# Order of the chunk work, PSUM tiles and side work in the first layer of a two-layer graph attention kernel

## Chip, cores and metric

The kernel runs on one core of a Trainium2 chip. The metric is the device time of one execution in microseconds (us), lower being better. A profile of a single execution is shown beside the timed runs; its times are those of that execution alone.

## What is computed

Two attention layers over 8 graphs of 2048 nodes with 256 features and 4 heads. Both layers normalise the rows, apply a ReLU, attend over the adjacency matrix and add the input back. The change concerns layer 0 only. Cut to what matters there:

```python
h = relu(layernorm(x))
q, k, v = (h @ W.T + b).reshape(B, N, H, 64)            # per head
kc, vc = k, v in chunks of 256 keys                      # 8 chunks
scores = clip(q @ kc.T / 8, -10, 10)
scores = where(mask == 0, -10, scores)
attn = softmax(scores, axis=-1)                          # over the 256 keys of ONE chunk
ctx = sum over chunks of attn @ vc
out = layernorm(ctx @ Wo.T + bo + h) * gamma + beta
x = x + out
```

The softmax is taken inside each chunk, so each chunk needs its own row sums before its context can be added up.

## The kernel before, in words

**Chunk steps.** Layer 0 is one loop (L701) over 256 steps n: 8 batches b, 4 query blocks qb of 512 rows, 8 chunks c of 256 keys. A chunk has four score tiles (two key tiles of 128 times two head pairs), each 128 keys by 2 heads by 512 queries. The loop is software-pipelined and written out by hand (`manual_schedule`, L87): every engine executes its instructions in the order in which Python emits them. In step n the scores of step n + 2 are made, the sums of step n + 1 and the contexts of step n.

**One score tile** (`scores`, L396): two matmuls with 64 rows of contraction, one per head, which share the array by rows (form 64\*128 in the profile), into one of two PSUM pairs of the tag "big" (two banks each). DVE then clips and masks the tile into SBUF (L409), and ACT exponentiates it (L415).

**Contexts** (`weigh`, L417): for a key tile and a half (`part`) of the value columns four matmuls with 32 output columns, one per head, which share the array by columns (form 128\*32). They accumulate over the two key tiles in the PSUM tile "both" (two banks, one per part).

**Sums**: GpSimd (POOL) adds the exponentials of the two key tiles (L695), four 128\*32 matmuls with a column of ones sum them over the partitions (`add_up`, L429) into the PSUM tile "sums". `divide` (L436) copies them with ACT to SBUF and sends them by DMA (SP queue) into a compact shape; `spread` (L444) takes the reciprocal on DVE and sends it through DRAM to all partitions as r. `accumulate` (L454) multiplies both by r on DVE (one instruction for both parts), and POOL adds the product to acc.

**Order in a step**: two score tiles, their exponentials; `advance` (only for n < 7); contexts of the first key tile; `advance`; two more score tiles; sums of step n + 1; contexts of the second key tile; last exponential and POOL's two sums; accumulate; spread; `advance`.

**Side work** hangs in generators in the list `aside`. One `advance` (L207) goes through the list and takes one piece of each generator, until a piece returns None, which marks work of TensorE in an "aux" PSUM tile. A piece that yields True has emitted something else, False means that it waits for its step. `drain` advances until a condition holds. The generators are:
- `make_limit` (L237), in the first steps: the adjacency matrix, loaded, cast and transposed on TensorE into the mask `limit`.
- `block` (L282), once for each 512 rows of a batch: `normal` (ACT makes h from x, L155), `turn` (four transposes on TensorE, form 128\*128, L167, and a copy to hT on ACT, L175), twice; then two aux tiles each for q, k, v (L164). The numbers in its `while` lines are the earliest steps.
- `statistics` (L131): the x blocks of a whole batch are loaded, and DVE takes row statistics (L47, L48); then each block is loaded a second time by `ahead`.
- `finish` (L461), for each query block: ACT makes h again (L472), the product with Wo in two aux tiles, DVE adds and row statistics, ACT (L506) and POOL (L475, L517) normalise and add, one POOL operation a step; a DMA stores x1.
- In the last batch `preparation` (L556) for layer 1, and `fill`.

PSUM before: big 2 pairs (4 banks), both (2), sums (1), aux (1).

Layer 1 (from L855) runs 512 rounds; its tiles `near` use the tag big, its row sums `den` the bank of sums.

Of the kernel before, what the change touches and what calls it, by code (L numbers as in the profile page):

```python
# [51 lines left out]
def layers(  # L52
# [36 lines left out]
    early, turns = [True], [0]  # L89

    def aux(dtype=F32):

        n = QB if dtype == F32 else 2 * QB
        turns[0] += 1
        if early[0] and turns[0] % 2:
            return psum.tile([P, 2 * n], dtype, tag="both", name="aux")[:, :n]
        return psum.tile([P, n], dtype, tag="aux", name="aux")
# [32 lines left out]

    def statistics(rows):  # L131

        rstd, off = norms()
        mv = small.tile([P, NKT, 2], F32, tag="mv", name="mv", bufs=1)
        for blk, xb in enumerate(ahead(rows)):
            if blk == 0:
                yield True
                yield True
            for t in range(NT):
                row_stats(nc, small, mv[:, blk * NT + t, :], xb[:, t, :])  # L140
                if t % 2:
                    yield True
        roots(mv, rstd, off, slice(0, NKT))
        yield True
        yield True
        return rstd, off
# [135 lines left out]
    def block(b, blk, xb, qs, ks, vs):  # L282
# [3 lines left out]
        while b and here[0] < first + (NCH, 2 * NCH, 3 * NCH, 4 * NCH - 2)[blk]:  # L286
            yield False
        while b == 1 and len(made) < NQB:
            yield False
        if b and blk == 0:  # L290
            yield True
        hT = big.tile([P, FC, QB], F32, tag="hT", name="hT", bufs=1)
        yield from block_turned(xb, blk, norm_of[b], hT)
        for name, to in (("q", qs), ("k", ks)):
# [4 lines left out]
            for oc in range(FC):  # L299
# [12 lines left out]
                if oc == FC - 1:  # L312
                    to.append(r)
                yield
        while b and here[0] < first + (0, 0, 3 * NCH + 2, 3 * NCH + 4)[blk]:
            yield False
        r = big.tile([P, NT, F], F32, tag="kv", name="v", bufs=12)
        for two in range(NT // 2):
            nc.scalar.copy(r[:, 2 * two : 2 * two + 2, :], sides(wT["v"], two, hT))
            if two == 1:  # L320
                vs.append(r)
            yield

    def batch(b):
        qkv[b] = ([], [], [])
        if b == 0:
            rstd, off = norms()
            mv = small.tile([P, NKT, 2], F32, tag="mv", name="mv", bufs=1)
            norm_of[b] = rstd, off
            for blk, xb in enumerate(ahead(x[b])):  # L330
                if blk == 0:
                    yield True
                for t in range(NT):
                    row_stats(nc, small, mv[:, blk * NT + t, :], xb[:, t, :])
                of = slice(blk * NT, (blk + 1) * NT)
                roots(mv, rstd, off, of)
                yield from block(b, blk, xb, *qkv[b])
        else:
            norm_of[b] = yield from statistics(x[b])
            for blk, xb in enumerate(ahead(x[b])):  # L340
                yield from block(b, blk, xb, *qkv[b])
# [54 lines left out]
    def scores(qb, kt, hp, qs, ks):  # L396

        ps = psum.tile([P, 2, QB], F32, tag="big", name="big", bufs=2)
# [55 lines left out]
    def accumulate(acc, both, r, first):  # L454

        to = acc if first else heads_tile("c", "c")
        nc.vector.tensor_tensor(to, both, bcast(r, 1, 2), ALU.mult)  # L457
        if not first:
            nc.gpsimd.tensor_tensor(acc, acc, to, ALU.add)  # L459
# [218 lines left out]
    def prepared(step):  # L678
# [3 lines left out]
        drain(lambda: qb in made and b in qkv and len(qkv[b][1]) > c // 2)  # L682
        qs, ks, _ = qkv[b]
        first = [scores(qb, 2 * c, hp, qs, ks) for hp in range(2)]
        for e in first:
            exponential(e)
        yield first
        second = [scores(qb, 2 * c + 1, hp, qs, ks) for hp in range(2)]
        exponential(second[0])
        yield second  # L690
        exponential(second[1])
        added = []
        for hp in range(2):
            both = heads_tile("add", "add")
            nc.gpsimd.tensor_tensor(both, first[hp], second[hp], ALU.add)  # L695
            added.append(both)
# [4 lines left out]
    for n in range(-2, len(steps)):  # L701
        here[0] = n
        more = n < NCH - 1
        coming = prepared(steps[n + 2]) if n + 2 < len(steps) else iter(())
        inside = -1 <= n < len(steps) - 1
        if n >= 0:
# [3 lines left out]
            if (qb, c) == (0, 2) and b + 1 < B:  # L710
# [4 lines left out]
            early[0] = False  # L715
            both = psum.tile([P, 2, QB], F32, tag="both", name="both")
        for k in range(2):
            weights.setdefault(n + 2, []).append(next(coming, None))
            if more:
                advance()  # L720
            if k == 1 and inside:
                sums = psum.tile([P, QB], F32, tag="sums", name="sums")
                add_up(weights[n + 1][2], sums)
                got = divide(sums)
            if n >= 0:
                weigh(2 * c + k, 0, weights[n][k], qkv[b][2], both, k == 0)
            if n >= 0:
                weigh(2 * c + k, 1, weights[n][k], qkv[b][2], both, k == 0)
            if k == 1:
                weights[n + 2].append(next(coming, None))  # L730
                if n >= 0:
                    if c == 0:
# [484 lines left out]
```

## Time and profile before

| what | us |
|---|---|
| median of 3 runs | 4355.52 (4352.07 to 4357.29) |
| the profiled execution, its own time | 4354.15 |
| its span, first to last instruction | 4352.4 |
| from the first row sum (L432) to the last product (L457) | 111.7 to 2842.9 |
| layer 1, from its first matmul (L786) | 2848.2 to the end |

| engine | busy us | share of the span |
|---|---|---|
| TensorE matmul (PE) | 4160.7 | 96% |
| GpSimd (POOL) | 3388.4 | 78% |
| VectorE (DVE) | 3188.1 | 73% |
| ScalarE (ACT) | 2522.3 | 58% |
| TensorE weight load (PEld) | 1364.8 | 31% |

A line of the profile names the engine, the line of the code, the operation, the tile it writes and the tiles it reads, the form of a matmul (rows\*columns of the array), the shape, and how often; then busy time and the mean of one. In the timeline the first number is the start in us from the span's start, the second the length, and a bracket holds idle time ahead of it and who ended it. An fp32 matmul appears as two instructions, each with its weight load. TensorE's matmuls overlap, so their starts say more than their lengths. A matmul of 512 columns starts 0.43 us after the one before it in the same part of the array.

### The profile page before, as it was taken

Reading aid. Unit: us, or ns where it says so; the run is one execution under the profiler, and the core shown is the slowest. Engines: PE = TensorE matmul, PEld = TensorE weight load, DVE = VectorE, ACT = ScalarE, POOL = GpSimd, SP = SyncE. Lnnn points to the kernel's source line nnn. Section 1 sums busy time; section 2 is a strip of 40 time slices with the busy share of each in tenths; the row PEclk is TensorE's granted clock in tenths of the full one; section 3 lists DMA queues with packets and bytes.
Section 4 is the critical chain, followed back from the end, with each engine's and each line's share of the span. In section 5 each row is a group of like instructions: output and inputs, shape, how many; then the busy total and the mean of one; then the engine's idle time right before and its main releaser. Section 6 shows DMA issues by size and latency. Waiting matters only on the chain. (4 is left out here: it accounts for less than half of the span.)

```text
span 4352.4 us, 85973 instructions
## 1 busy us (share of the span) xinstructions
PE 4160.7 (96%) x34742; PEld 1364.8 (31%) x34742; DVE 3188.1 (73%) x3718; ACT 2522.3 (58%) x3194; POOL 3388.4 (78%) x1711
## 2 busy tenths in 40 slices
PE   6799999999999999999999999989999999999998
PEld 2233323323323323333333323323333232333322
DVE  3876666676676675676676667679888898989897
ACT  4455555555555555555555557655656656566665
POOL 0477787787787777887877788888888888888897
PEclk9899999999999999999999999999999999999999
DMA  2321122121121121121121112122221212122121
GB/s 72 125 79 46 41 61 58 37 65 54 41 66 46 48 66 42 46 63 51 42 67 52 41 49 60 39 79 57 60 62 48 69 44 78 50 61 69 32 59 35
DMA packets 278152, 246.03 MB, mean 57 GB/s; under 512 B 95728, under 2 KB 228592, under 8 KB 277744
## 3 DMA queue, kind: packets, MB, share of 16 engines
q1 hardware_dynamic: 273136, 223.67, 18.2%
q0 software_dynamic: 4608, 16.78, 1.0%
q8 instruction: 274, 4.49, 0.4%
q14 instruction: 134, 1.10, 0.1%
HBM read 202.05 MB, written 36.18 MB: 55 GB/s over the span
## 5 line engine op out<-in xcount | busy, mean ns | idle before, releaser
L695 POOL TENSOR_TENSOR add<-E 128x1024 f32<-128x1024 f32 x512 | 1204.0, 2374 | 617.2 <-ACT E L415 562.8
L415 ACT ACTIVATE E<-E 128x1024 f32<-128x1024 f32 x1024 | 1081.6, 1058 | 970.7 <-DVE E L409 942.5
L409 DVE SCALAR_TENSOR_TENSOR E<-big,limit 128x1024 f32<-128x1024 f32 x1024 | 1199.1, 1212 | 444.3 <-PE big L401 325.7
L775 DVE SCALAR_TENSOR_TENSOR e<-near,far,limit 128x1024 f32<-128x1024 f32 x1024 | 1239.8, 1277 | 40.3 <-POOL t L892 19.4
L892 POOL TENSOR_TENSOR t<-t,e 128x1024 f32<-128x1024 f32 x448 | 1054.9, 2389 | 222.0 <-ACT t L888 185.2
L401 PE MATMUL big<-qT,kT 64*128 64x512 f32 x4096 | 1042.1, 623 | 33.6 <-DVE E L409 33.4
L786 PE MATMUL acc<-e,qn 128*32 128x512 f32 x8192 | 1041.3, 597 | 6.9 <-DVE e L775 6.7
L421 PE MATMUL both<-E,v 128*32 128x512 f32 x8192 | 990.5, 597 | 0.2 <-DVE c L457 0.2
L888 ACT ACTIVATE t<-e,quot 128x1024 f32<-128x1024 f32 x512 | 561.8, 1142 | 275.0 <-PE den L798 166.2
L401 PEld LDWEIGHTS big<-qT,kT 64*128 64x128 f32 x4096 | 350.6, 187 | 621.2 <-issue 360.5
L459 POOL TENSOR_TENSOR acc<-acc,c 128x1024 f32<-128x1024 f32 x224 | 533.4, 2381 | 2.7 <-DVE c L457 2.7
L457 DVE TENSOR_TENSOR c<-both,r 128x1024 f32<-128x1024 f32 x224 | 274.3, 1224 | 243.7 <-PE both L421 129.0
L421 PEld LDWEIGHTS both<-E,v 128*32 128x32 f32 x8192 | 242.7, 110 | 654.9 <-issue 546.9
L786 PEld LDWEIGHTS acc<-e,qn 128*32 128x32 f32 x8192 | 267.3, 110 | 515.2 <-issue 465.5
L798 PE MATMUL den<-t,for_sums 128*32 128x512 f32 x2048 | 366.4, 597 | 57.0 <-POOL t L892 56.3
L432 PE MATMUL sums<-add,ones 128*32 128x512 f32 x2048 | 284.9, 608 | 3.0 <-POOL add L695 2.6
L798 PEld LDWEIGHTS den<-t,for_sums 128*32 128x32 f32 x2048 | 78.4, 109 | 273.6 <-POOL t L892 171.6
L155 ACT ACTIVATE h<-x,off,rstd 128x256 f32<-128x256 f32 x256 | 139.2, 592 | 29.0 <-DMA x<-in_x_dram 18.7
L439 ACT COPY s<-sums 128x512 f32<-128x512 f32 x256 | 145.2, 567 | 7.9 <-PE sums L432 7.9
L446 DVE RECIPROCAL sum<-sum 128x16 f32<-128x16 f32 x256 | 64.2, 251 | 95.7 <-DMA sum<-s 95.3
L164 PE MATMUL aux<-hT,wq 128*32 128x512 f32 x1024 | 128.0, 622 | 2.7 <-ACT hT L175 2.7
L164 PE MATMUL aux<-wo,acc 128*32 128x256 f32 x2048 | 122.3, 379 | 0.8 <-ACT hT L175 0.8
(116 smaller groups left out, 2910.6 us busy)
## 6 DMA issues: line engine op xcount, KB each, us to landing
r<-inv SPq DMA_DIRECT2D x1024, 64.0 KB
x<-in_x_dram SPq DMA_DIRECT2D x92, 512.0 KB
es<-er SPq DMA_DIRECT2D x64, 512.0 KB
adj_in<-in_adj_dram SPq DMA_DIRECT2D x32, 512.0 KB
x<-o POOLq DMA_DIRECT2D x32, 512.0 KB, 3.3
x<-x SPq DMA_DIRECT2D x32, 512.0 KB
xh<-x SPq DMA_DIRECT2D x64, 256.0 KB
out_dram<-xh SPq DMA_DIRECT2D x64, 256.0 KB
```

Source lines behind the costliest of these rows:

```text
L401: nc.tensor.matmul(ps[:, hh, :], ks[kt // NT][own, hp, (kt % NT) * P : (kt % NT + 1) * P], qs[qb][own, hp, :], start=True, stop=True,)
L409: nc.vector.scalar_tensor_tensor(e, ps, -0.5, bcast(limit[:, qb, kt, :], 1, 2), ALU.max, ALU.min)
L415: nc.scalar.activation(e, e, AF.Exp, scale=0.25 * EDGE)
L421: nc.tensor.matmul(both[32 * h : 32 * h + 32, part, :], vs[kt // NT][:, kt % NT, mine], es[h // 2][:, h % 2, :], start=first, stop=not first,)
L432: nc.tensor.matmul(sums[32 * h : 32 * h + 32, :], ones, es[h // 2][:, h % 2, :], start=True, stop=True)
L459: nc.gpsimd.tensor_tensor(acc, acc, to, ALU.add)
L695: nc.gpsimd.tensor_tensor(both, first[hp], second[hp], ALU.add)
L775: nc.vector.scalar_tensor_tensor(e, near[hh], far[:, jt, h : h + 1], limit[:, 2 * half : 2 * half + 2, jt, :], ALU.max, ALU.min,)
L786: nc.tensor.matmul(acc[32 * q : 32 * q + 32, blk, :], qn[jt // NT][:, jt % NT, hp * P + 32 * q : hp * P + 32 * q + 32], es[q // 2][:, blk, :],
L798: nc.tensor.matmul(den[32 * q : 32 * q + 32, :], for_sums[:, m, 2 * hp + q // 2, :], ts[q // 2][:, q % 2, :], start=(m == 0 and k == 0), s ...
L888: nc.scalar.activation(t, now[hh], AF.Copy, scale=quot[:, jt // 2, h : h + 1])
L892: nc.gpsimd.tensor_tensor(ts[hh], ts[hh], now[hh], ALU.add)
```

## The change

Layer 0 is reordered and its PSUM is dealt out anew; the arithmetic stays.
- PSUM: "big" gets three pairs, taken in turn by `pair()`. The tiles sums and aux are gone: each takes the first half of the next pair. In layer 1 three fixed pairs serve: two for `near`, the third for `den` (first bank) and aux (second bank).
- Order in a step: contexts of the first key tile; all four score tiles in one run, two exponentials; sums of step n + 1; two exponentials and POOL's sums; contexts of the second key tile; accumulate; spread; then all side work of the step.
- Side work: after `spread` up to three calls of `advance`, until 3 aux tiles are used (n < 16), or 2 (n < 32, and the steps called `late`), or 1 (all others).
- `accumulate` multiplies the two parts in two instructions.
- A block's x is loaded once. Its statistics are an own generator, appended to `aside` when the load is issued; `following()` loads the next block after the second `turn` of the block before it. New earliest steps; the order is k, v, q instead of q, k, v (block 2 keeps q, k, v).
- The first scores no longer wait for all blocks of batch 0, but q of the block is awaited as well.

```diff
+    def pair(dtype=F32):
+        n = QB if dtype == F32 else 2 * QB
+        return psum.tile([P, 2, n], dtype, tag="big", name="big", bufs=3)
     def aux(dtype=F32):
-        n = QB if dtype == F32 else 2 * QB
-        turns[0] += 1
-        if early[0] and turns[0] % 2:
-            return psum.tile([P, 2 * n], dtype, tag="both", name="aux")[:, :n]
-        return psum.tile([P, n], dtype, tag="aux", name="aux")
+        used[0] += 1
+        return rest[0][:, 1, :] if rest else pair(dtype)[:, 0, :]
...
-    def block(b, blk, xb, qs, ks, vs):
+    def block(b, blk, xb, following, qs, ks, vs):
...
+        def due(*slots):
+            return b == 0 or here[0] >= first + slots[blk]
...
+        while not due(0, NCH - 2, 2 * NCH - 2, 3 * NCH + 1):
+            yield False
         hT = big.tile([P, FC, QB], F32, tag="hT", name="hT", bufs=1)
         yield from block_turned(xb, blk, norm_of[b], hT)
+        following()
+        for name in ("qkv" if blk == 2 else "kvq"):
+            while not due(*{
+                "k": (0, 0, 3 * NCH - 1, 3 * NCH + 1),
+                "v": (0, 0, 3 * NCH + 1, 3 * NCH + 3),
+                "q": (NCH - 2, 2 * NCH - 2, 3 * NCH - 2, 4 * NCH - 2),
+            }[name]):
+                yield False
...
     def batch(b):
         qkv[b] = ([], [], [])
+        rstd, off = norm_of[b] = norms()
+        mv = small.tile([P, NKT, 2], F32, tag="mv", name="mv", bufs=1)
+        coming, counted, loaded = [], set(), []
+        def statistics(blk, xb):
+            for t in range(NT):
+                row_stats(nc, small, mv[:, blk * NT + t, :], xb[:, t, :])
+                if b and t % 2:
+                    yield True
+            roots(mv, rstd, off, slice(blk * NT, (blk + 1) * NT))
+            if b:
+                yield True
+            counted.add(blk)
+        def following():
+            blk = len(loaded)
+            if blk < NQB:
+                xb = load(x[b], blk)
+                loaded.append(blk)
+                coming.append(xb)
+                aside.append(statistics(blk, xb))
+        following()
         if b == 0:
...
+            following()
+        yield True
+        for blk in range(NQB):
+            while blk not in counted:
+                yield False
+            yield from block(b, blk, coming.pop(0), following, *qkv[b])
...
     def accumulate(acc, both, r, first):
         to = acc if first else heads_tile("c", "c")
-        nc.vector.tensor_tensor(to, both, bcast(r, 1, 2), ALU.mult)
+        for part in range(2):
+            nc.vector.tensor_tensor(to[:, part, :], both[:, part, :], r, ALU.mult)
...
-        first = [scores(qb, 2 * c, hp, qs, ks) for hp in range(2)]
-        for e in first:
+        tiles = [[scores(qb, 2 * c + k, hp, qs, ks) for hp in range(2)] for k in range(2)]
+        for e in tiles[0]:
             exponential(e)
-        yield first
-        second = [scores(qb, 2 * c + 1, hp, qs, ks) for hp in range(2)]
-        exponential(second[0])
-        yield second
-        exponential(second[1])
+        yield tiles
+        for e in tiles[1]:
+            exponential(e)
...
+            def contexts(k):
+                for part in range(2):
+                    weigh(2 * c + k, part, weights[n][0][k], qkv[b][2], both, k == 0)
+            contexts(0)
+        coming = prepared(steps[n + 2]) if n + 2 < len(steps) else iter(())
+        weights[n + 2] = [next(coming, None)]
+        inside = -1 <= n < len(steps) - 1
+        if inside:
+            sums = pair()[:, 0, :]
+            add_up(weights[n + 1][1], sums)
+            got = divide(sums)
+        weights[n + 2].append(next(coming, None))
+        if n >= 0:
+            contexts(1)
...
+            accumulate(accs[qb], both, r, c == 0)
...
+        if inside:
+            r = spread(got)
+        used[0] = 0
+        late = n < 0 or qb == NQB - 1 or (qb == NQB - 2 and c > NCH - 3) or (qb == 0 and c < 4)
+        for _ in range(3):
+            if used[0] < (3 if n < NQB * NCH // 2 else 2 if n < NQB * NCH or late else 1):
                 advance()
```

## The prediction

> **What bounds the kernel now.** First the busy times: TensorE 96%, no other engine over 78%. Then the three stages by windows: 0 to 324 us (start, with the masks), 324 to 2842 (layer 0 from step 16), the rest (layer 1). The page's first lines and the middle stage:
>
> ```profile
> span 4352.4 us, 85973 instructions
> ## 1 busy us (share of the span) xinstructions
> PE 4160.7 (96%) x34742; PEld 1364.8 (31%) x34742; DVE 3188.1 (73%) x3718; ACT 2522.3 (58%) x3194; POOL 3388.4 (78%) x1711
> ...
> 324.00:2842.00 2518.00, 2473.40 (x19386) 800.80 (x19382) 1645.78 (x2170) 1431.26 (x1814) 1991.09 (x991) 1.00 0.18 52
> ```
>
> In the middle stage TensorE is idle 2518.0 - 2473.4 = 45 us. So a step costs what TensorE's own stream costs, and only what shortens that stream, or makes it wait, counts. Its weight loads show the price of changing between forms of the array:
>
> ```profile
> 1506.22 0.13 PEld L164 LDWEIGHTS aux<-hT,wq 128*32 128x32 f32 x4 [0.30 <-issue]
> 1506.65 0.13 PEld L164 LDWEIGHTS aux<-hT,wq 128*32 128x32 f32 x4 [0.30 <-issue]
> 1507.62 0.30 PEld L401 LDWEIGHTS big<-qT,kT 64*128 64x128 f32 x4 [0.84 <-DVE sum L446]
> 1508.16 0.19 PEld L401 LDWEIGHTS big<-qT,kT 64*128 64x128 f32 x2 [0.24 <-issue]
> 1508.59 0.19 PEld L401 LDWEIGHTS big<-qT,kT 64*128 64x128 f32 x2 [0.23 <-issue]
> 1509.54 0.16 PEld L421 LDWEIGHTS both<-E,v 128*32 128x32 f32 x8 [0.76 <-issue]
> 1509.99 0.13 PEld L421 LDWEIGHTS both<-E,v 128*32 128x32 f32 x4 [0.30 <-issue]
> ```
>
> Loads of one form follow each other every 0.43 us: that is one slot. From 1506.65 to 1509.99 seven slots pass (one of q, four of scores, two of contexts), 3.01 us; it took 3.34. The excess, 0.33, is one visit to the 64\*128 form; I use 0.34, from the matmul starts. Check: a step without side work has 8 + 8 + 2 slots and two visits, 7.73 + 0.68 = 8.41; the sums start at 2753.05 and again at 2761.45, 8.40 apart.
>
> **The saving.** One visit a step goes: a bare step becomes 18 x 0.43 + 0.34 = 8.07. Steps 16 to 253 still make scores: 238 x 0.34 = **-80 us**.
>
> One part goes the other way. A `turn` (form 128\*128) stood between contexts and scores; now it stands between 128\*32 forms. That is one change more than before for 62 turns, at a third to a half of 0.34 (one of a visit's two changes): **+8 us**. [...]
>
> **The new step, from rows.** Let T be the first score load.
> - Scores take 3.63. DVE's first tile starts 1.25 after T (1507.62 to 1508.87 in the timeline), one takes 1.22 and they follow every 1.14 to 1.18: ends at T + 2.47, 3.6, 4.75, 5.9. The fourth score tile takes the first's pair at 2.7, the sums the second's at 3.65: both just free. I put **+8 us** for 0.03 a step; bounds 0 and 0.1 a step (24).
> - ACT: two exponentials (1.06 each) to 4.7, copy of the sums to 5.35, two exponentials to **7.4**.
> - Contexts end at **6.26**. DVE's halves cost 0.68 each (L493 and L832, same 128x512 from PSUM: 678 and 682 ns) and end at 6.5 and 7.1; 0.14 a step more DVE work, hidden while DVE has slack. With an aux tile (four slots, 1.72) next nothing waits. In a bare step the next contexts wait for the first half: 0.4. Were the halves released together it would be 1.0.
> - Reciprocal: in before it starts 1.87 after the copy ends, so at 7.25 to 7.5. DMA inv, then r, lands near 12.5; the next product wants it at 14 or later. Covered.
> - POOL's two sums (2.37 each) run from 6.5 to 11.2; the next step's add_up wants them at 8.07 + 3.65 = 11.7 or later. Covered, with 0.5 to spare in bare steps.
>
> So side work begins at 6.26 on TensorE, while ACT is bound to this step's exponentials to 7.4 and DVE to 7.5. In before a piece and the next one lay four or more us of TensorE work apart; now they follow at once.
>
> **What the side work then waits for.** Following the generators step by step for n = 16 to 255 gives these cases (in batch 4, steps 128 to 159: first turns at 130, 139, 150; load at 130; bare 128, 136, 149, 156).
> - *A. `normal` and its `turn` in one step, 21 times*: the first advance emits h and returns True, so the second emits the transposes. h (0.55 each) starts at 7.4, the transposes end at 9.1 instead of 7.0: 2.1. In 11 of them `finish` has put four more ACT operations ahead (four L472 or L506 take 2.06): 4.2. 10 x 2.1 + 11 x 4.2 = 67. Behind the waiting transposes stand the next contexts and scores, and for those wait DVE and ACT.
> - *B. Both turns in one step, 8 times*: copy hT 0.57, then h again: 1.9 each, 15.
> - *C. `turn` and then k or q at once, 10 times*: hT copied only after 7.4: 1.1 each, 11. Drains ahead of scores (k of block 3), 5 times: 0.57 or 0.69 plus semaphores: 7.
> - *D. Loads, 6 times*: `following` issues x, and the next advance emits its statistics. On SP the load is queued behind the four r DMAs (to 10.75), and lands 3.3 later (below), so at 14.05. DVE, in order, has statistics of 4 x 0.55 to take then, to 16.3, ahead of the next score tiles, which wanted it at 9.7: 6.5 us, 4 times; 3.0 twice: 32.
>
> ```profile
> DMA to landing us min/median/max: 3.2/3.3/8.5
> ```
>
> - *E. Other DVE work after 7.5 that is not done when the next scores come (statistics of x and of `finish`, 1.1 a pair), 12 times*: 13. Bare steps, 31 x 0.4: 12.
> - *F. ACT's `fill` and POOL's doubled roots (1.04 of L127 a block)*: I put 10; bounds 0 and 30.
>
> A to F: 67 + 15 + 11 + 7 + 32 + 13 + 12 + 10 = 167, with the 8 above 175.
>
> **A stall costs its length and then the clock.** Before has this once in full:
>
> ```profile
> 1627.43 1.90 PE L421 MATMUL both<-E,v 128*32 128x512 f32 x16
> 1631.96 1.01 PE L167 MATMUL aux<-ident,h 128*128 128x128 f32 x4 [2.63 <-ACT h L155]
> 1632.89 3.56 PE L401 MATMUL big<-qT,kT 64*128 64x512 f32 x8
> ...
> 1631.31 1.09 ACT L155 ACTIVATE h<-x,off,rstd 128x256 f32<-128x256 f32 x2 [4.05 <-DMA x<-in_x_dram]
> ...
> 1622.00:1632.70 10.70, 8.02 (x56) 2.19 (x54) 6.26 (x7) 4.49 (x7) 5.51 (x3) 1.00 0.42 126
> 1632.70:1636.10 3.40, 3.40 (x10) 1.19 (x8) 0.40 (x2) 3.40 (x6) 2.62 (x2) 0.50 0.02 2
> ```
>
> h is late, the transposes wait 2.63, and then a granted clock of 0.50 for 3.4 us makes eight scores take 3.56 instead of 1.99: 1.6 more. In the middle stage six transposes waited 1.4 to 2.7; three were followed by such a window (615.5, 953.4, 1632.7). I price 1.6 at half the waits near 2 (10 of A, 8 of B) and at all longer ones (11 of A, 6 of D): 26 x 1.6 = **+42 us**; bounds 0 and 35 x 1.6 = 56.
>
> [...]
>
> **What is removed.** The old waits: 45 idle and three half-clock windows of 1.6: **-50 us**, since the new order deals all of them anew. The second load of x is off the critical path: nothing.
>
> **The start** (to step 16 at 317.6 by the old step length). Scores start after two blocks of batch 0 instead of four: first scores near 76 instead of 100. But the two blocks' aux tiles then stretch steps -2 to 4 to 9 to 15 us, and the masks (24 tiles, 2.4 us of DVE each, L251 and L266) bind DVE later instead of sooner, with fetch, cast and transpose in one step twice (n = 6, 10: about 9 us). My sum, step by step, is 320: **0**, bounds -25 and +25.
>
> **Layer 1**: same banks in number, den and aux in separate banks as before; nothing. Bounds ±8 (0.5% of its 1510).
>
> **Sum**: -80 + 8 - 50 + 175 + 42 + 0 = +95. Waits in neighbouring steps overlap (a step held up by A or D gives DVE, ACT and POOL time to catch up); I take a tenth of 217 off, 20. So +75, on the profiled execution's own 4354.15 (span 4352.4 and 1.75 around it; the median of the runs, 4355.52, is 1.4 above): **4430 us**.
>
> **Rivals.**
> 1. *Faster*: the transposes do not wait for ACT, because h is ready or ACT is free by 6.3. For: ACT is busy only 58%, and its 7.4 rests on the sums' copy standing ahead of two exponentials; against: ACT executes in order, and in the timeline the copy at 1504.74 stands between exponentials as emitted. Then A, B and their clock (67 + 15 + 32) go: 95 - 114 = -19, and if D goes too (with 10 of clock) -61: **4290 to 4335**. It decides when all the new waits, clock included, come to less than the 122 saved.
> 2. *Slower still*: the run of four is bound by DVE in most steps. The fourth tile's pair is free at 2.47 and wanted at 2.25 if its weights are to be loaded ahead, and any DVE work left over at T + 1.25 shifts it. At 0.3 a step more, 238 x 0.3 = +71: **4500**. For: no cover; against: mean DVE load is 65% in the middle stage.
> 3. *It doesn't do what it says*: side work is not spread (31 steps bare, 83 with two) and the saving and the waits cancel: **4355**, when the waits come to about 122, a little over half of my 217.
>
> **How the numbers follow.** Forecast, 4380 to 4480: 0.58. Rival 1: 0.24. Rival 2: 0.12. Rival 3: 0.06. Slower by over 0.2% (8.7 us, about what a measurement of this kernel can tell from no change): 0.58 + 0.12 = 0.70; faster 0.24; same 0.06. The range leaves a tenth at each end: from 4305, inside rival 1, to 4510, just beyond rival 2; the bounds of the clock, the start and the run's 0.1 lie within.
>
> **What would show it.** Right: weight loads of scores in runs of four tiles with one gap of about 0.5 on either side, bare steps near 8.1 to 8.5; TensorE idle ahead of transposes, ended by ACT h L155, 60 us or more in all; DVE idle ahead of statistics until a DMA of x; more half-clock windows than three in the middle stage; layer 0 ending near 2918. Wrong: idle of TensorE in layer 0 below 100 us, or waits of scores for DVE E in most steps, or a layer 1 that differs from 1510.

## The result, and the profile after

The changed kernel takes **4586.49 us** (median of 4 runs, 4585.19 to 4588.04) against 4356.41 for the kernel before (4 runs): 1.053 times as long, 95% interval 1.0512 to 1.0549. The forecast was 4430, with a range up to 4510. The direction was right, the loss is three times as large: 232 us instead of 75.

The head of the page after (span; busy times):

```profile
span 4586.2 us, 86733 instructions
## 1 busy us (share of the span) xinstructions
PE 4150.5 (90%) x34742; PEld 1497.1 (33%) x34742; DVE 3197.8 (70%) x3974; ACT 2523.2 (55%) x3194; POOL 3406.5 (74%) x1795
```

TensorE has the same 34742 matmuls and nearly the same busy time (4160.7 before). What is new is time in which it stands still. The windows show where; the columns are length, then busy us and instructions of PE, PEld, DVE, ACT and POOL, then the granted clock, the DMA share and GB/s. The rows are layer 0 from step 16, and layer 1:

```profile
358.40:3075.00 2716.60, 2463.40 (x19276) 915.26 (x19278) 1659.35 (x2431) 1431.96 (x1813) 2010.68 (x1074) 0.97 0.16 43
3075.00:4586.00 1511.00, 1428.57 (x13502) 480.00 (x13494) 1339.40 (x1291) 933.36 (x1182) 1257.89 (x636) 0.99 0.20 58
```

Layer 1 keeps its 1510 us, as predicted. In layer 0 TensorE is idle 2716.6 - 2463.4 = 253 us where it was idle 45, and the clock is 0.97 where it was 1.00. By the sums of each step the loss divides into three: step 16 begins at 358.5 instead of 323.6 (+35), steps 16 to 231 take 2441.5 instead of 2281.7 (+160), and from there to the last sums 265.0 instead of 225.8 (+39).

The saving is there all the same. Steps with two aux tiles and nothing to wait for take 11.55 to 11.63 where they took 11.84 to 11.86, and the run of sixteen score matmuls takes 3.70. That is about 0.24 a step, not the full 0.34. What stands against it is seen in single steps. First a bare step (one without an aux tile) of the timeline (start, length, engine, line; in brackets the idle time ahead and who ended it):

```profile
2456.32 1.93 PE L431 MATMUL both<-E,v 128*32 128x512 f32 x16
2458.31 1.29 DVE L469 TENSOR_TENSOR acc<-both,r 128x512 f32<-128x512 f32 x2 [0.72 <-PE both L431]
2459.74 1.92 PE L431 MATMUL both<-E,v 128*32 128x512 f32 x16 [1.50 <-DVE acc L469]
2461.60 0.70 PE L411 MATMUL big<-qT,kT 64*128 64x512 f32 x2
```

The two products (x2, 1.29 together) begin only when the last of the sixteen context matmuls has ended, although half of them wrote the first half. The next contexts begin only when both products have ended. So the step takes 9.9, not 8.4.

Next a block whose `normal` is emitted at the end of step 187 and both turns in step 188:

```profile
2309.12 4.62 DVE L419 SCALAR_TENSOR_TENSOR E<-big,limit 128x1024 f32<-128x1024 f32 x4 [3.09 <-PE big L411]
2309.14 2.36 POOL L471 TENSOR_TENSOR acc<-acc,c 128x1024 f32<-128x1024 f32 x1
2311.58 0.23 POOL L129 TENSOR_SCALAR rstd<-mv 128x4 f32<-128x4 f32 x1
...
2313.32 0.20 POOL L132 TENSOR_TENSOR off<-off,rstd 128x4 f32<-128x4 f32 x1
...
2313.55 1.09 ACT L141 ACTIVATE h<-x,off,rstd 128x256 f32<-128x256 f32 x2 [6.23 <-POOL off L132]
...
2314.55 1.99 ACT L425 ACTIVATE E<-E 128x1024 f32<-128x1024 f32 x2
...
2318.04 4.66 POOL L705 TENSOR_TENSOR add<-E 128x1024 f32<-128x1024 f32 x2 [4.53 <-ACT E L425]
...
2319.94 1.18 PE L153 MATMUL big<-ident,h 128*128 128x128 f32 x4 [4.80 <-ACT h L141]
```

Read it from the top. GpSimd comes to the roots only behind its adding to acc. VectorE makes the step's four tiles E from 2309.12 to 2313.74, so the first is ready near 2310.3. ScalarE has h at the head of its queue and waits 6.23 us for the roots, until 2313.55; this step's exponentials (L425), the first of them ready some 3 us before the end of that wait, stand behind h and start at 2314.55. (In the eight such steps this wait of ScalarE is 6.2 twice, 10.2 to 10.6 five times and 13.7 once.) So GpSimd's sums, which need the exponentials, come late too, and so do the copy of hT and the second h, which stand behind those exponentials; for that h TensorE waits 4.80. Before this wait ends the clock is halved (window view, granted clock third from the end):

```profile
2318.60:2325.40 6.80, 5.46 (x22) 1.68 (x24) 0.25 (x1) 2.36 (x5) 6.80 (x4) 0.50 0.20 40
```

Third, the start (a mask tile in step 6). SyncE's queue holds the four r DMAs, which wait for the reciprocal on its way through DRAM (inv is issued from 201.75, r from 203.16); the adjacency blocks are issued behind them, from 204.92, and the cast, the transposes and TensorE wait for the block:

```profile
203.16 1.72 SPq L461 DMA_DIRECT2D r<-inv  x4
...
204.92 6.15 SPq L230 DMA_DIRECT2D adj_in<-in_adj_dram  x4
...
209.52 1.04 ACT L236 CAST masks<-adj_in 128x1024 bf16<-128x1024 int32 x1 [8.51 <-DMA adj_in<-in_adj_dram]
210.62 1.03 PE L251 MATMUL big<-identb,masks 128*128 128x128 bf16 x8 [10.47 <-ACT masks L236]
```

### The profile page after: what moved, and what is told of

Its sections match the earlier page's. It is cut to its first block, busy times and chain, and to the rows that moved or that the text cites. A ratio compares the mean times of both kernels' runs of the same rounds, so it can differ in the third digit from the quotient of the medians.

```text
span 4586.2 us, 86733 instructions
## 1 busy us (share of the span) xinstructions
PE 4150.5 (90%) x34742; PEld 1497.1 (33%) x34742; DVE 3197.8 (70%) x3974; ACT 2523.2 (55%) x3194; POOL 3406.5 (74%) x1795
## 5 line engine op out<-in xcount | busy, mean ns | idle before, releaser
L425 ACT ACTIVATE E<-E 128x1024 f32<-128x1024 f32 x1024 | 1053.7, 1056 | 1007.7 <-DVE E L419 989.8
L787 DVE SCALAR_TENSOR_TENSOR e<-big,far,limit 128x1024 f32<-128x1024 f32 x1024 | 1239.5, 1275 | 37.0 <-POOL t L906 19.0
L411 PE MATMUL big<-qT,kT 64*128 64x512 f32 x4096 | 974.4, 613 | 65.1 <-DVE E L419 63.3
L469 DVE TENSOR_TENSOR c<-both,r 128x512 f32<-128x512 f32 x448 | 288.7, 686 | 195.0 <-PE both L431 94.3
L810 PE MATMUL big<-t,for_sums 128*32 128x512 f32 x2048 | 360.2, 598 | 59.0 <-POOL t L906 50.8
L442 PE MATMUL big<-add,ones 128*32 128x512 f32 x2048 | 283.9, 618 | 9.1 <-POOL add L705 0.2
L153 PE MATMUL big<-ident,h 128*128 128x128 f32 x512 | 101.2, 317 | 143.5 <-ACT h L141 137.3
L449 ACT COPY s<-big 128x512 f32<-128x512 f32 x256 | 149.8, 585 | 83.2 <-PE big L442 83.2
L810 PEld LDWEIGHTS big<-t,for_sums 128*32 128x32 f32 x2048 | 76.5, 109 | 278.6 <-POOL t L906 168.8
L153 PEld LDWEIGHTS big<-ident,h 128*128 128x128 f32 x512 | 56.9, 151 | 256.4 <-ACT h L141 193.0
L150 PE MATMUL big<-hT,wk 128*32 128x512 f32 x1024 | 123.5, 609 | 12.0 <-ACT hT L161 12.0
```

Of the source, the lines that this page charges most:

```text
L411: nc.tensor.matmul(ps[:, hh, :], ks[kt // NT][own, hp, (kt % NT) * P : (kt % NT + 1) * P], qs[qb][own, hp, :], start=True, stop=True,)
L425: nc.scalar.activation(e, e, AF.Exp, scale=0.25 * EDGE)
L469: nc.vector.tensor_tensor(to[:, part, :], both[:, part, :], r, ALU.mult)
L787: nc.vector.scalar_tensor_tensor(e, near[hh], far[:, jt, h : h + 1], limit[:, 2 * half : 2 * half + 2, jt, :], ALU.max, ALU.min,)
L810: nc.tensor.matmul(den[32 * q : 32 * q + 32, :], for_sums[:, m, 2 * hp + q // 2, :], ts[q // 2][:, q % 2, :], start=(m == 0 and k == 0), s ...
```

## The experiments

Theory: three separate losses, each one rule of waiting. (1) The halves are tied by their common tile (TensorE's wait of 1.50 above). (2) Links of one chain across engines (load, statistics, roots, h, transposes) are emitted in one place, with no other work to cover the latency, and an engine that keeps to the order of emission, as ScalarE does above for 6.23 us, carries the wait to work that has nothing to do with it. (3) At the start the same holds for SyncE's queue (TensorE's 10.47 above). Rivals: an engine that is simply full (VectorE, ScalarE), or the three shared PSUM pairs.

"Step 16" below is the start of its sums, "middle" the time from there to step 231, and half-clock windows are stretches with a granted clock of 0.50. Ratios are against the kernel before. The edits are shown cut to the lines that matter, against the changed kernel if nothing else is said.

**e1: the halves in two tiles.**

```diff
-            both = psum.tile([P, 2, QB], F32, tag="both", name="both")
+            both = [psum.tile([P, QB], F32, tag=f"both{p}", name=f"both{p}") for p in range(2)]
```

> The changed kernel with the two halves of the contexts in two PSUM tiles of one bank each, not in one tile of two banks; all else as it is. In the changed kernel a bare step takes 9.81 to 9.94 us, and the next contexts start 1.5 us after TensorE came free, when the second of the two products has ended; neither product starts before the last context matmul of both halves has ended. Theory 1 (the tile, not the half, is what is released and waited for): the first product then starts about 0.9 us sooner, the next contexts wait for one product of 0.68 alone, bare steps fall to 8.4 to 8.6, steps with a turn from 9.94 to about 8.9, total 50 to 80 us below the 4586.5 of the changed kernel (31 x 1.4 + 45 x 0.5 to 1.0, minus what other waits take back). Rival (DVE itself, bound by its four score tiles and two products, sets a floor of 9.9 a step): bare steps stay at 9.8 to 9.9 and the total within 10 us of 4586.5.

The edit splits layer 1's accumulator in the same way; its time stays within 1 us. 4545.68 us (ratio 1.0446, 1.0415 to 1.0476): 41 less than the changed kernel. In the bare step the next contexts now follow without a stop (x32 in one run), and the next scores begin 3.77 after the contexts instead of 5.28:

```profile
2427.51 3.84 PE L431 MATMUL both<-E,v 128*32 128x512 f32 x32
2428.69 1.50 DVE L469 TENSOR_TENSOR acc<-both,r 128x512 f32<-128x512 f32 x2
2431.28 3.27 PE L411 MATMUL big<-qT,kT 64*128 64x512 f32 x14
```

Most bare steps take 8.30 to 8.47, and steps with one turn, 9.94 where nothing else held them up, take 8.9 to 9.4: theory 1, and no floor set by VectorE. The total falls by 41 and not by the 50 to 80 expected. One part of that is seen: the 8 steps with both turns, each next to a bare one, became 11 us longer, as if the lost time had covered part of the wait for h.

**e2: `normal` a step after the roots.**

```diff
+            at = here[0]
...
-            counted.add(blk)
+            counted[blk] = at
...
-            while blk not in counted:
+            while blk not in counted or (b and here[0] <= counted[blk]):
```

> The changed kernel, but a block's first `normal` waits for a step later than the one in which GpSimd's roots of its statistics were issued. Theory 2 (ScalarE, in order, stands still with h at its head until GpSimd, which takes the roots behind its sums and its adding to acc, is done; the exponentials behind h, and with them GpSimd's sums of the next step, slip): the 8 steps with both turns, now 9 us over the bare sum each (75.8 in all), fall to 2 to 4 over it, ScalarE's idle time before h on GpSimd's off falls from 110 us to under 30, and the total falls by 40 to 60 us. Rival (the transposes wait because ScalarE still has two exponentials and the operations of finish ahead of h, whatever GpSimd does): these steps keep 7 to 9 us, idle time moves to another line, the total stays within 10 us of 4586.5.

4554.68 (1.0466, 1.0436 to 1.0497), 32 less. ScalarE's wait for off falls from 110.0 to 19.5 us, and half-clock windows in layer 0 from 184 to 140. But the 8 steps still take 6.1 over the bare sum, not 2 to 4: `normal`, both turns and often two operations of `finish` now meet in one step. The rival has that part.

**e3: statistics two steps after their load.**

```diff
-        def statistics(blk, xb):
+        def statistics(blk, xb, at):
+            while b and here[0] < at + 2:
+                yield False
...
-                aside.append(statistics(blk, xb))
+                aside.append(statistics(blk, xb, here[0]))
```

> The changed kernel, but the row statistics of a block of x are taken at the earliest two steps after its load was issued. Theory 3 (VectorE, in order, waits for the load that is queued behind the DMAs of r, and the next score tiles wait behind it; each such wait also sets the matmul clock to half for some time): the 6 steps with a load, now about 8 to 10 us over the bare sum, fall to 1 to 2 over it, total lower by 40 to 55 us, of which about a third is clock. Rival (the statistics, 4 x 0.55 us, cost VectorE the same wherever they stand, since it is bound in these steps by its own work): at most 10 us.

4552.16 (1.0461, 1.043 to 1.0491), 34 less, and half-clock windows 143. VectorE's 35.2 us of waiting for x are gone. It is less than expected because waits came up elsewhere: step 99, a drain, goes from 7.8 over the bare sum to 13.2, and steps 49 and 76, which had waited for nothing of the kind, have 7 to 8 each.

**e4: the order of the chunk alone**, with the side work of the kernel before: one `advance` between `contexts(0)` and the score run, one behind `spread`, and its generators `block`, `statistics`, `batch` (`more` holds for n < 7).

```diff
             contexts(0)
+        for _ in range(2 if more else 1):
+            advance()
         coming = prepared(steps[n + 2]) if n + 2 < len(steps) else iter(())
...
-        used[0] = 0
...
-        for _ in range(3):
-            if used[0] < (3 if n < NQB * NCH // 2 else 2 if n < NQB * NCH or late else 1):
-                advance()
+        for _ in range(2 if more else 1):
+            advance()
```

> The order of the chunk alone: all four score tiles in one run, three PSUM pairs in turn, the product in halves; but the side work as in the kernel before (a batch's statistics in one generator, x loaded twice, the old earliest steps, one piece between the two contexts' score run and one at the end of the step, two each in the first steps). Theory (the spreading and placing of the side work costs what was lost, the order of the chunk gains what was forecast): the 80 us of the saved visits stay, the waits for h, roots and loads in the middle stage go; bare and nearly bare steps still pay 1.5 to 1.8 for the products that are released together; total 4340 to 4420. Rival A (the three pairs, without a bank of their own for sums and aux, are what costs): 4480 or more, TensorE idle over 150 us in the middle stage. Rival B (all costs lie in the side work, none in the order): 4290 or less.

4543.48 (1.0441, 1.041 to 1.0471): a miss, within rival A's bounds: TensorE is idle 231 us from step 16 on. The half-clock windows are nearly gone (27 us), yet the middle takes 2411, for bare steps take 9.93 there too.

**e5: e4 with the halves in two tiles** (the edit of e1).

> The order alone (e4_order_alone) with the two halves of the contexts in two one-bank PSUM tiles. e4_order_alone has no half-clock windows to speak of (27 us against 184 in the changed kernel) and still took 4543; between step 16 and step 231 its steps without an aux tile take 9.93, its steps with little work 10.42 to 10.52, where the kernel before has 8.40 and 9.2 to 9.6. Theory (nearly all that this order loses in the middle is the wait for both halves): bare steps 8.3 to 8.5, steps 16 to 231 in 2260 to 2300 us instead of 2411 (before: 2282), total 4390 to 4425; the rest over before lies in the first 16 steps (about 38 longer than before) and in the last batch (about 15). Rival (the three pairs shared with sums and aux tiles hold PE up as well): steps 16 to 231 in 2340 or more, total 4460 or more.

4462.11 (1.026, 1.0243 to 1.0277): both numbers lie within the rival's bounds. Most bare steps fall to 8.3 or 8.4 as expected, but the middle takes 2345. So the common tile cost this order 81 us, and something else remains. One wait of it, here and in the kernel before:

```profile
DVE o L494 <- POOL o L476: 174.7, 31, 6.0
```

```profile
DVE o L493 <- POOL o L475: 50.8, 22, 2.9
```

The columns are us in all, times, longest. The piece of `finish` ahead of the scores makes VectorE wait for GpSimd, and all four score tiles stand behind it, where in the kernel before only two did. Whether this wait is what is lost, e10 asks.

**e6: e1, e2 and e3 together.**

> The changed kernel with three repairs together: two one-bank tiles for the halves, the first `normal` of a block a step after its roots, the statistics two steps after their load. Alone they gave 41, 32 and 34 us. If the three losses lie in different steps (bare and turn steps, steps of a block's turns, steps of a load), the sum holds: 4586 - 107 = 4480, within 15. If they share steps, so that one repair hides behind the other, 4500 to 4520. If the wait for both halves had also been slack that let other waits catch up, more than the sum: 4450 to 4465.

4488.42 (1.0317, 1.0297 to 1.0338): 98 less, where the three alone gave 107. So the losses lie in different steps for the most part.

**e7: the fetches of the masks on ScalarE's queue.**

```diff
-            nc.sync.dma_start(raw, adj[q0 : q0 + P, half * 1024 : (half + 1) * 1024])
+            nc.scalar.dma_start(raw, adj[q0 : q0 + P, half * 1024 : (half + 1) * 1024])
```

> The changed kernel, but the adjacency blocks of the masks are fetched by DMAs issued on ScalarE's queue, not on SyncE's. In the changed kernel three fetches of a step are emitted behind `spread`, so SyncE issues them behind the four r DMAs (r at 203.16 to 204.88 us, fetches from 204.92, the cast waits until 209.52, TensorE 10.47). Theory (SP's queue, in order behind r, is what makes the masks late at the start): fetches leave 3 to 4 us sooner in some eight steps, step 16 begins 20 to 35 us sooner (358.5 now, 323.6 before), total 4550 to 4568. Rival (the masks cost their 2.4 us of VectorE each, and the bytes themselves, whatever the queue): step 16 within 5 us of 358, total 4580 to 4592. A loss is possible if ScalarE stands still at a fetch that waits for its buffer: then step 16 begins later than 365.

4567.73 (1.05, 1.0479 to 1.0521), 19 less; step 16 begins at 341.4 instead of 358.5, 17 sooner where 20 to 35 were expected. A step like the one above, with the fetches ahead of r:

```profile
200.89 0.97 ACTq L230 DMA_DIRECT2D adj_in<-in_adj_dram  x2
...
206.54 1.03 PE L251 MATMUL big<-identb,masks 128*128 128x128 bf16 x8 [5.03 <-ACT masks L236]
```

TensorE waits 5.03 instead of 10.47. The 17 us are half of the 35.

**e8: a step between the links.** The pieces are the same; only when a generator may go on is changed, between steps 16 and 223. (Blocks may start one to three steps earlier and k two, statistics stand at the head of the list, two steps more of a query block take two aux tiles, and loads of x and the o tiles of `finish` wait until a buffer is free. The run doesn't separate these from the spacing that they serve.)

```diff
+            if not free and spent.get(steps_of) == here[0]:
+                continue
             got = next(steps_of, aside)
...
+            if got in ("h0", "h1"):
+                later(steps_of)
...
         hs = normal(xb, blk, 0, norm)
-        yield True
+        yield "h0"
         turn(hs, 0, hT)
         hs = normal(xb, blk, 1, norm)
-        yield
+        yield "h1"
...
-                aside.append(statistics(blk, xb))
+                aside.insert(0 if b else len(aside), statistics(blk, xb))
+                later(aside[0])
...
-        while not due(0, NCH - 2, 2 * NCH - 2, 3 * NCH + 1):
+        while not due(0, NCH - 3, 2 * NCH - 4, 3 * NCH - 2):
```

> The changed kernel, but between steps 16 and 223 a block gives no second piece in the step in which its `normal` was emitted, the statistics of x begin at the earliest a step after the load, and so that this still ends in time statistics stand at the head of the list, blocks and k may start one to three steps earlier and two more steps take two aux tiles. By the emitted order a `normal` with its own turn in one step falls from 21 to about 3, both turns in one step from 8 to 2, statistics in the step of their load from 6 to 2, steps without an aux tile from 26 to 18, drains from 4 to none. Theory (what was lost in the middle is links of one chain across engines emitted with no other work between them): of the 221 us over the bare sum in those steps 130 to 180 go, half-clock windows fall from 184 us to under 80, steps 16 to 231 fall from 2441 to 2270 to 2320, total 4410 to 4460. Rival (the side work waits because the engines behind it are too busy at the end of a step, wherever it stands): the waits move to other steps, total 4530 or more.

4419.17 (1.0157, 1.0138 to 1.0175): 167 less than the changed kernel, with nothing taken away. Layer 0 from step 16, and TensorE's wait for h (137.3 in the changed kernel, over 43 waits):

```profile
371.30:2909.00 2537.70, 2407.71 (x19288) 910.30 (x19292) 1656.59 (x2424) 1429.51 (x1813) 2010.66 (x1071) 0.99 0.16 46
```

```profile
PE big L156 <- ACT h L144: 26.1, 9, 7.9
```

The middle falls from 2441.5 to 2277.1, half-clock windows from 184 to 27. All engines have about the busy times they had (VectorE 3196.7 of 3197.8, GpSimd 3407.4 of 3406.5): no engine was full. Bare steps still take 9.9, but there are 21 in the middle instead of 27. The start is not better: step 16 begins at 371.3, 13 later than in the changed kernel.

**e9: e8 with the edits of e1 and e7.**

> e8_spaced with the halves in two one-bank tiles and the adjacency fetches on ScalarE's queue. If the three causes are separate, their gains add: e8_spaced less 41 less 19, so 4350 to 4400 if e8_spaced comes out at 4410 to 4460; below 4345 it would beat the kernel before. If the steps without an aux tile that e8_spaced has lost already take away what two tiles gain, less 25 to 30 only.

**4339.27** (0.9971, 0.9961 to 0.998): 80 less than e8, where e1 and e7 alone gave 60, and 0.3% faster than the kernel before. The middle takes 2231.2, 50 less than before: here part of the forecast's saving shows. Its steps are still 80 us over the prediction's own sum for them (8.07 and the aux tiles), where the kernel before's are 55 over theirs (8.41); so the visits' 73 us (215 steps at 0.34) are there, and 25 of them go in waits. The three shared PSUM pairs are still there, so they are not what cost the time. What is left over before is the start (step 16 at 348.2 against 323.6) and the last batch (238.1 against 225.8).

**e10: e5 with the first piece behind the second exponentials** (edit against e5).

```diff
             contexts(0)
-        for _ in range(2 if more else 1):
-            advance()
...
         weights[n + 2].append(next(coming, None))
+        for _ in range(2 if more else 1):
+            advance()
         if n >= 0:
             contexts(1)
```

> e5_order_two_tiles with its first piece of side work not between the contexts of the first key tile and the score tiles, but behind the second pair of exponentials, ahead of the contexts of the second key tile. In e5 VectorE waits 170 us for GpSimd's o ahead of its add of `finish` (30 times, up to 6.0), with the four score tiles queued behind it; the steps with it take 13.0 to 14.2, in the kernel before 10.7 to 11.9. Theory (what e5 still loses in the middle, 2345 against 2282, is a wait on VectorE ahead of the scores): these steps fall to 10.3 to 11.2, steps 16 to 231 to 2265 to 2300, total 4375 to 4425. Rival (the piece waits there as well, and the contexts and products behind it): 4450 or more.

4479.05 (1.0294, 1.0275 to 1.0313): a miss. VectorE's wait for GpSimd's o is gone, but the time is not. Now transposes wait 52 us for h (33 in e5) and the middle takes 2382. Only the start gains: step 16 at 334.1, in e5 352.1. So what e5 loses in the middle (63 us over the kernel before) has no shown cause; these runs say only that the old side work doesn't fit the new order in either place.

**e11: the kernel before with the edit of e7 alone.**

> The kernel before with the adjacency fetches on ScalarE's queue alone. In it casts and minima wait 27 us for fetches in the first steps, and 30 us of TensorE's idle time there stand behind a cast. If the fetches that are queued behind r are what the masks wait for here too: step 16 begins 8 to 20 us sooner, total 4332 to 4344. If VectorE's 2.4 us for each mask tile sets the pace there, or ScalarE stands still at the fetches: 4348 to 4360.

4360.34 (1.002, 1.0011 to 1.0029): slightly slower. There two of a step's three places for side work lie ahead of its r DMAs, which may be why the queue was no limit. The loss lies in the start (first sums at 115.5 instead of 111.7, step 16 at 329.6 instead of 323.6); its cause is not shown.

**e12: e9, all blocks of batch 0 first** (edit against e9).

```diff
-        drain(lambda: qb in made and b in qkv and len(qkv[b][1]) > c // 2 and len(qkv[b][0]) > qb)
...
+            and len(qkv[b][0]) > (qb if b else NQB - 1)
```

> e9_spaced_all, but the first scores wait for all four blocks of batch 0, as in the kernel before. Step 16 begins at 348.2 in e9, at 323.6 before. In e9 and in the changed kernel the blocks of batch 0 and the 24 mask tiles lie in the steps, TensorE busy 135 of 168 us from 180 to 348 at granted clocks of 0.87 and 0.94. Theory (what is left of the late start is that blocks are made inside the first steps, and push the masks into steps 5 to 14): the first sums come at 112 to 120, steps 0 to 7 take 14 to 16 each with three mask tiles, the next eight 8.4 to 10, step 16 begins at 322 to 336, total 4312 to 4328. Rival (the masks cost the same wherever they stand, since cast, transpose and VectorE's two operations follow each other in one place of the step): step 16 within 6 us of 348, total 4333 to 4345.

4351.40 (0.9996, 0.9986 to 1.0005): a miss of both. The first sums come at 124.1, step 16 at 368.1. Starting on two blocks makes step 16 about 20 sooner (12 in the total), so it is not the cause.

**e13: e9 with one piece ahead of `contexts(1)` in steps 0 to 15.**

> e9_spaced_all, but in steps 0 to 15 one of the pieces of side work stands behind the second pair of exponentials, ahead of the contexts of the second key tile; up to two more stay at the end. e10 moved pieces to that place too, and there step 16 began at 334.1 instead of 352.1 (e5). Theory (what is left of the late start is that fetch, cast, transposes and VectorE's two operations of three mask tiles follow each other in one place, with nothing of the chunk to cover them): step 16 begins 10 to 20 us sooner than e9's 348.2, total 4318 to 4330. Rival (e10's gain came from the place of other pieces, or from its two pieces more a step): step 16 within 5 us of 348, total 4334 to 4345.

4333.04 (0.996, 0.9946 to 0.9974), the fastest kernel of this case. Step 16 at 345.0: within the rival's bound, not the theory's; the total lies 1 us below the rival's.

**e14: e9 with a step between the links in the last batch too.**

> e9_spaced_all, but in the last batch VectorE's four sums of the products of w and a come at the earliest a step after GpSimd's product, and the blocks of the preparation for layer 1 a step after the roots. In e9 VectorE waits 7.79 us for such a product (scores behind it 7.30), ScalarE 12.53 for off; the last batch takes 238.1 from step 231, and steps 228 and 230 take 17.15 and 16.86. Theory (the same loss as in the middle: links of one chain in one place): steps 228 and 230 fall to 10 to 12, total 8 to 15 us lower, 4324 to 4331. Rival (in the last batch VectorE and GpSimd have too much to do, and the waits only move): total 4334 to 4345.

4336.68 (0.9966, 0.9954 to 0.9979). Steps 228 and 230 fall from 17.15 and 16.86 to 8.74 and 8.39, but steps 235, 244 and 248 then take 17.1 to 19.7 (8.8 to 10.2 in e9). The waits move; here the rival is right.

## Why the prediction was wrong, step by step

For each step from 16 to 252, its length less 8.07 and its aux tiles (1.72 each, 0.78 for a turn), summed by the prediction's own cases, comes to 348.4 us. The half-clock loss, counted as half the windows' length, is taken out of each case and has a row of its own. The measured figure of the first row is therefore a sum, not a measurement of the saving:

| step of the prediction | forecast | measured |
|---|---|---|
| layer 0 from step 16 without waits (2507.5 before, less 80, plus 8, less 50) | 2385.5 | 2706.5 - 348.4 = 2358.1 |
| A, `normal` and its turn (21) | 67 | 71.5 |
| B, both turns (8) | 15 | **39.9** |
| bare steps (27 without a load) | 11 (0.4 each) | **59.8** (2.2 each) |
| D, loads | 32 | 29.0, and part of A |
| C, drains, E, F, and the 8 | 49 | 56 |
| half clock | 42 | **92.2** |
| overlap | -20 | none seen |
| start | 0 (bounds ±25) | **+35** |
| layer 1 | 0 | +1 |

The four bold rows are (39.9 - 15) + (59.8 - 11) + (92.2 - 42) + 35 = 159, and 232 - 75 = 157. The other rows cancel to within 3.

Two of the rows need care. Half of the windows' length is an upper figure for the clock: TensorE is busy for 126 of the 184 us of windows, and half of that is 63. The other 29 are waits, above all of B, which then comes to 56. And of the bare steps 25 have 1.7 to 1.9 each, 45.5 together; the other two, 232 and 235 of the last batch, have 7.6 and 6.7, and there VectorE waits for GpSimd (9.5 us in step 232).

- **The step "in a bare step the next contexts wait for the first half: 0.4. Were the halves released together it would be 1.0" failed**, and twice. The halves are released together (both in one tile), and moreover the first product waits for all contexts, not for its own half: 1.5 and more. The alternative of 1.0 stood in the text, but was priced from the product's end alone and not carried into the bounds. In 25 steps this was 1.8 each instead of 0.4. e1 shows it: 9.88 to 8.4, so 1.5 is the common tile's and 0.3 the wait that was forecast. Steps whose only work aside is a turn lost 1.1 for the same reason, which the sum had at nothing.
- **B at 1.9 each failed.** I counted ScalarE's own work (copy, then h) and took the roots to be there. They stand behind GpSimd's adding to acc, and that wait, 6.2 to 13.7, falls on exponentials queued behind h. The steps wait 5.0 to 7.0 each, by the two ways of counting the clock. e2 shows the part of the roots; in e8, with a step in between, no step of the middle has both turns.
- **The clock at 1.6 a wait failed.** The number of windows was right (26 priced, 27 seen), their length was not: all three of before's were 3.4 us long, and I took that as the cost of a wait. Here the mean is 6.8, and the loss 63 to 92 instead of 42, above the bound of 56.
- **The start at 0 failed.** My sum counted VectorE's 2.4 us a tile and overlooked that the fetches move behind the r DMAs on SyncE's queue: the queue was not in the sum. e7 shows 17 of the 35. For the rest, tried on e9, making all blocks first (e12) is worse and another place for the tiles (e13) gives 3; it stays open. Half-clock windows ahead of step 16 take 82 us, in the kernel before 41, so up to 20 of the 35 may be clock that follows these waits; no run separates it.
- **The last batch** (+39) had no term of its own; its waits stand in the rows above. In the trace VectorE waits for GpSimd's products (9.5 us in step 232) and ScalarE for a load of x1 (5.3 in step 236), which looks like the same kind. e14 doesn't settle it, and the cause stays open.
- **Right** were D, layer 1, and A in its sum: transposes waited 1.4 or 3.4 in most of its steps, where 2.1 and 4.2 were forecast, but two waited 4.2 to 4.5, and one in the last batch 9.4. The saving is there, at about 0.24 a step where nothing waits; the sum put 0.34 less 0.03.

Of the rivals, 1 was wrong: transposes wait 137 us for h. Rival 2 was wrong: scores wait for VectorE in 15 steps only, 63 us in all. Rival 3 had waits that cancel the saving; they came to far more.

In step 188 ScalarE kept to the order of emission: it stood for 6.23 us with h at its head, the last 3 of them with a tile for the exponentials behind it ready.

## What to carry to other kernels

Side work is not free because its engine has time: count how far apart in the program the links of its chain stand, on every engine and queue that they pass (here 6.23 us of ScalarE in step 188, 10.47 us of TensorE in step 6). One place for all side work puts all links side by side; a step between them, with the earlier starts that this takes, gave 167 us back here without removing work. And splitting an operation to release a buffer earlier gained nothing here while both parts shared the tile that is waited for (bare steps of 9.9, in e1 with two tiles mostly 8.30 to 8.47).

## What the runs showed of the hardware

- In layer 0 of the changed kernel from step 16 the half-clock windows came in multiples of 3.4 us. There are 27: eight of 3.4, twelve of 6.8, six of 10.2, one of 13.7. None of 43 waits of TensorE between 1.2 and 1.8 us was followed by one. Of the 34 over 1.9, all but four had one begin during the wait or within 3.5 us after it, and three of these four fell into a window that was already running. In the kernel before, from step 16 on, two waits of 1.6 were followed by one and three of 2.2 to 2.3 were not, and in its start three waits of 1.5 were followed by one, so in these two traces the border lies at about 2 us and is not sharp.
- The length was not given by one wait alone: waits of 2.0 to 2.3 us were followed by windows of 3.4 to 10.2. Only one of these six waits, of 2.15, stands alone, and its window has 3.4; in the other five a second wait of 4.6 to 5.8 us overlaps the window. What else sets the length stays open. They cost 63 to 92 us here, about a fifth to a quarter of all that steps took above their sum.
- A fetch on ScalarE's queue took its place in ScalarE's order: in e7 one was issued from 206.75 for 0.33 us, between a cast that ended at 206.48 and the next, which began at 207.13.
